# A graph network with a selecting LSTM: layer norm by node tile, and the weight loads and logit stores around the recurrence reordered

## The chip, the cores and the metric

The kernel runs on one core of one Trainium2 chip. The metric is the device time of one execution in microseconds (us), less is better. In the profile PE is TensorE (PEld its weight loads), DVE is VectorE, ACT is ScalarE, POOL is GpSimd and SP is SyncE. A name with a q (SPq, ACTq, POOLq) is the part of that engine which issues DMAs.

## What is computed

Eight residual blocks are applied one after another to a node matrix x of 625 x 512 fp32. Each block takes the layer norm of x over its 512 columns, computes something, and adds the result to x, so that no block can begin its own matmuls before the last one has finished x:

```python
def _layernorm(x, axis=-1, eps=1e-05):
    m = jnp.mean(x, axis=axis, keepdims=True)
    v = jnp.var(x, axis=axis, keepdims=True)
    return (x - m) / jnp.sqrt(v + eps)

x = x + _L0_gnn_ref(_layernorm(x), edge_index, ...)      # Chebyshev graph convolution, 8 terms
x = x + _L0_ffn_ref(_layernorm(x)[None], ...)[0]         # one of 16 experts, chosen by the mean node
x = x + _L1_gnn_ref(_layernorm(x), edge_index, ...)      # weighted graph convolution, 20000 edges
x = x + _L1_ffn_ref(_layernorm(x)[None], ...)[0]         # 8 experts, gates by Sinkhorn, each takes its top 78 nodes
x = x + _L2_gnn_ref(_layernorm(x), ...)                  # 32 relations from 8 bases, sum over 20000 edges
x = x + _L2_ffn_ref(_layernorm(x)[None], ...)[0]         # LSTM over the 625 nodes, 4 weight sets
x = x + _L3_gnn_ref(_layernorm(x), edge_index, ...)      # two graph attention layers
x = x + _L3_ffn_ref(_layernorm(x)[None], ...)[0]         # grouped-query attention, one of 3 variants
```

The sixth block is a recurrence. For each of the 625 nodes in order it picks one of four weight sets by the largest of four logits, which depend on the last hidden state, the last cell state and the node:

```python
def step(carry, x_t):
    h, c = carry
    sel_in = jnp.concatenate([h, c, x_t], axis=-1)
    logits = sel_in @ W_sel.T + b_sel
    onehot = jax.nn.one_hot(jnp.argmax(logits, axis=-1), Sx)
    g_all = x_t @ W_ih.T + h @ W_hh.T + b_ih + b_hh      # for all four sets
    g = jnp.einsum('bsg,bs->bg', g_all, onehot)
    h2, c2 = _lstm_activate(g, c)
    return (h2, c2), h2
```

## The kernel before

The 625 nodes are five tiles of 125 partitions (`P`, `NT`). x stays in SBUF as 125 x 5 x 512 for the whole run. The edges are 160 chunks of 125 (`EC`). The stages are methods called in order: `setup` (which calls `graph`, counting matrices over the edges), then `l0_gnn`, `l0_ffn`, `l1_gnn`, `l1_ffn`, `l2_gnn`, `l2_ffn`, `l3_gnn`, `l3_ffn`, then `store`. A scheduler puts the instructions of each engine in an order of its own and adds the semaphores for what depends on what. Only the regions marked `tc.tile_critical()` are ordered by hand: the loops over edge chunks and the recurrence. Such a region begins when every engine and every transfer before it is done, which the profile shows as a wait of SP (L174, L286, L744, L1038).

**Layer norm.** `layer_norm` (L39 to L55) is called at the head of each stage. It takes bn_stats and bn_aggr of the five tiles on DVE (L46, L47), one square root of 125 x 5 values on ACT (L48), one reciprocal (L49) and five scalings on DVE (L51). The results go to a pool of the stage. `transpose_nodes` (L57 to L64) then turns each tile by four PE transposes (L63) into one PSUM tile, which DVE copies (L64).

**l1_ffn** first asks ACT for eight 1 MB loads of `bases` (L531), for the next stage. It multiplies all nodes by the experts in (expert, tile) products of four fp32 matmuls (L551, `products`). The first five experts' products (`EARLY`) are held in SBUF (`y_early`, L560) while Sinkhorn (L574 and after) and the ranking run. The ranking takes one row of gates per expert through PE (L595) and compares it on DVE (L602, L604). Then each product is scaled by its selected gate and added to x (L620), and with each product of a later expert two held ones are added as well.

**l2_gnn** loads the small combination matrix in sixteen DMAs on ACT (L648), forms the node's eight basis products (L668), combines them to 32 relations (L694) and stores each relation's table to DRAM in 1 MB stores (L703). The relational sum is a hand-ordered region: POOL gathers 125 rows per chunk by an indirect DMA into one of six slots (L748), DVE builds the weighted one-hot matrix (L752), PE sums into five PSUM banks (L216).

**l2_ffn** has two parts. The gate phase computes all gates from the nodes: eight blocks c of W_ih, each as two 1 MB loads on ACT (`load`, L810) into the memory of the fourth recurrent set, `whh[3]`, of which two blocks have room; five tiles each; per (c, t) ten matmuls (L907, L909), then the gates are split into three bf16 summands (`summands`, L797 to L800) and stored to DRAM as `gxp` by SP (L920, 750 KB). Beside it the cell is computed as if each node stood alone (`cell_alone`, `turn`, `parts`), which gives the node's own logits. The recurrent sets 0 to 2 are loaded by SP in twelve 1 MB pieces (`load_set`, L767), one at every odd tile; set 3 by POOL after the last two blocks. At the end the logit rows `xl3` are stored into the last 26 columns of `gxp` by five DMAs of 19 KB on ACT (L938), and the recurrence (L950 on) loads one row of `gxp` per step (`gs`, L1152), adds the recurrent matmuls (L1024) and applies the cell on DVE and ACT.

The `gxp` columns that no logit fills are zeroed by 15 small DMAs on POOL (L92). `store` (L343) writes x with one 1.25 MB DMA.

## Time and profile before

| | |
|---|---|
| runs shown | 5628.12, 5625.29, 5628.01 us; median 5628.01 |
| profiled execution | 5631.39 us, its span 5629.6 us, mean granted TensorE clock 0.946 |
| PE busy | 4921.4 us, 87% of the span |
| DVE busy | 2534.5 us, 45% |
| ACT busy | 1099.2 us, 20% |
| POOL busy | 346.7 us, 6% |
| DMA | 243.7 MB, mean 43 GB/s |

| stretch of the span (us) | what runs |
|---|---|
| 0 to 181 | setup and graph |
| 181 to 505 | l0_gnn |
| 505 to 558 | l0_ffn |
| 558 to 779 | l1_gnn |
| 779 to 976 | l1_ffn |
| 976 to 1208 | l2_gnn to the last relation's table |
| 1242 to 1503 | relational sum |
| 1503 to 1884 | norm and gate phase of l2_ffn |
| 1909 to 5046 | recurrence |
| 5046 to 5391 | l3_gnn |
| 5391 to 5630 | l3_ffn and the store |

The profile is one execution taken by the hardware profiler. A timeline row gives start, length, engine, line of the kernel, operation, output<-input and count; in brackets at its end stands how long the engine had been idle before it, and what it was waiting for. Rows of a queue (ACTq, SPq) have the time that the engine spent on issuing those DMAs, waits included. A row of busy tenths gives one digit for each fortieth of the span.

### The profile page before, as it was taken

The page shows a single profiled execution, that of the slowest core. Times are in us where ns is not written, and L with a number is a line of the kernel's source. Part 1 is how long each engine was busy: PE and PEld are TensorE (multiplying, and loading weights), DVE is VectorE, ACT ScalarE, POOL GpSimd, SP SyncE. Part 2 cuts the span into 40 slices and gives each one's busy share as a digit, 9 for nine tenths or more (in the row PEclk, how much of TensorE's full clock was granted, in tenths as well). Part 3 has the DMA queues.
Part 4 walks back from the last instruction along what each step waited for, and adds up shares of the span by engine and source line. Part 5 has one row for each costly group of instructions (what it writes and reads, how often), then busy time and mean ns, then how long its engine had stood idle before and what let it go on. Part 6 is the DMA issues. An engine that isn't in the chain of part 4 may idle for free.

```text
span 5629.6 us, 171946 instructions
## 1 busy us (share of the span) xinstructions
PE 4921.4 (87%) x73432; PEld 2934.8 (52%) x73433; DVE 2534.5 (45%) x10389; ACT 1099.2 (20%) x3500; POOL 346.7 (6%) x297
## 2 busy tenths in 40 slices
PE   6898678967799699898999999999999898888887
PEld 2444453322344366565666666666666565565543
DVE  6312637234334344444454445444555444456514
ACT  1000731210033111111111111111111111114314
POOL 1000620017500000000000000000000000000000
PEclk8798889979899899999999999999999999999989
DMA  1000121686554200000000000000000000011000
GB/s 15 32 30 12 37 95 38 185 251 166 140 160 146 75 10 11 10 11 10 11 11 10 10 11 11 11 10 10 11 10 11 10 11 10 9 33 38 16 32 10
DMA packets 148634, 243.70 MB, mean 43 GB/s; under 512 B 55035, under 2 KB 57412, under 8 KB 146342
## 3 DMA queue, kind: packets, MB, share of 16 engines
q1 hardware_dynamic: 83850, 163.27, 9.8%
q0 software_dynamic: 45168, 51.96, 3.7%
q10 hardware_dynamic: 19372, 25.52, 1.5%
q8 instruction: 115, 1.88, 0.2%
q14 instruction: 129, 1.06, 0.1%
HBM read 156.40 MB, written 73.72 MB: 41 GB/s over the span
## 4 chain that ended last, share of the span: by engine, by line
PE 54%; DVE 6%; issue 3%; DMA 2%; PEld 1%; ACT 1%; PEldq 0%; SPq 0%; ACTq 0%; DVEq 0%
PE gate_if L1024 22%; PE gate_o L1024 9%; PE gate_g L1024 9%; DVE to L1136 3%; PE gate_if L1015 3%; PE idle L1032 2%; DMA gs<-gxp 2%; PE o_ps L1197 2%; PE o_ps L1263 2%; PE big_ps L1372 1%; PE big_ps L1392 1%; PE gate_g L1015 1%; PE gate_o L1015 1%; PE fc_ps L1303 1%; PE blk_ps L1253 0%
## 5 line engine op out<-in xcount | busy, mean ns | idle before, releaser
L1024 PE MATMUL gate_if<-whh,h 128*32 128x256 f32 x21664 | 1349.6, 388 | 0.0
L1024 PEld LDWEIGHTS gate_if<-whh,h 128*32 128x32 f32 x21664 | 600.1, 109 | 365.6 <-DVE h L1140 129.0
L1024 PE MATMUL gate_g<-whh,h 128*32 128x128 f32 x19968 | 673.9, 275 | 1.5 <-issue 1.5
L1127 DVE STREAM_TRANSPOSE tif<-gate_if 128x256 f32<-128x256 f32 x625 | 281.3, 450 | 840.6 <-PE gate_g L1024 837.1
L1024 PE MATMUL gate_o<-whh,h 128*32 128x128 f32 x19968 | 659.2, 273 | 0.0
L1024 PEld LDWEIGHTS gate_g<-whh,h 128*32 128x32 f32 x19968 | 521.9, 110 | 176.0 <-issue 166.8
L1024 PEld LDWEIGHTS gate_o<-whh,h 128*32 128x32 f32 x19968 | 557.9, 110 | 0.0
L1119 ACT ACTIVATE sd<-tif 128x8 f32<-128x8 f32 x625 | 134.7, 216 | 2124.7 <-DVE tif L1127 2124.7
L1015 PE MATMUL gate_if<-gs,pick 128*128 128x256 bf16 x678 | 192.6, 284 | 138.3 <-DVE to L1136 46.2
L907 PE MATMUL gx_ps<-whh,xT 128*125 128x512 f32 x640 | 299.9, 612 | 0.3 <-DVE xls L847 0.3
L216 PE MATMUL acc<-msg,dst_w 125*125 125x512 f32 x352 | 188.4, 640 | 107.2 <-DMA msg<-rel_table,row_i 94.4
L1128 DVE STREAM_TRANSPOSE tg<-gate_g 128x128 f32<-128x128 f32 x625 | 198.0, 317 | 163.5 <-PE gate_g L1024 163.5
L748 POOL DMA_INDIRECT msg<-rel_table,row_i x160 | 196.5, 1228 | 550.0 <-issue 536.9
L1136 DVE STREAM_TRANSPOSE to<-gate_o 128x128 f32<-128x128 f32 x625 | 197.9, 317 | 66.3
L1084 PE MATMUL logits<-gs,three 128*2 128x5 bf16 x624 | 103.5, 166 | 130.1 <-issue 50.9
L1148 DVE MAX8 mx<-logits 2x8 f32<-2x8 f32 x624 | 101.1, 162 | 248.0 <-PE logits L1096 248.0
L1032 PE MATMUL idle<-hot 128*128 128x384 bf16 x624 | 204.7, 328 | 0.0
L1084 PEld LDWEIGHTS logits<-gs,three 128*2 128x2 bf16 x624 | 49.3, 79 | 291.5 <-DMA gs<-gxp 229.4
L1015 PEld LDWEIGHTS gate_if<-gs,pick 128*128 128x128 bf16 x678 | 65.0, 96 | 227.3 <-DVE to L1136 138.8
L907 PEld LDWEIGHTS gx_ps<-whh,xT 128*125 128x125 f32 x640 | 115.6, 191 | 128.0 <-issue 127.2
L216 PEld LDWEIGHTS acc<-msg,dst_w 125*125 125x125 f32 x352 | 57.3, 192 | 239.1 <-issue 192.6
L752 DVE TENSOR_SCALAR dst_w<-iota,dst,ew 125x625 f32<-125x625 f16 x160 | 106.7, 669 | 160.6 <-PE acc L216 145.3
(377 smaller groups left out, 6380.9 us busy)
## 6 DMA issues: line engine op xcount, KB each, us to landing
rel_table<-h_rel SPq DMA_DIRECT2D x39, 1024.0 KB
gs<-gxp SPq DMA_DIRECT2D x625, 48.6 KB
gxp<-gxo SPq DMA_DIRECT2D x40, 750.0 KB
whh<-in_L_ffn_W_ih ACTq DMA_DIRECT2D x16, 1024.0 KB
whh<-in_L_ffn_W_hh SPq DMA_DIRECT2D x12, 1024.0 KB
node_basis<-by_basis SPq DMA_DIRECT2D x39, 256.0 KB
ch_wk<-in_L_gnn_weight SPq DMA_DIRECT2D x8, 1024.0 KB
expert<-in_L_ffn_experts SPq DMA_DIRECT2D x8, 1024.0 KB
```

The source lines that it names most:

```text
L216: m = PE.matmul(out, lhs, rhs, start=False, stop=False, skip_group_check=True)
L748: get = nc.gpsimd.indirect_dma_start(out=msg[:, i, :], out_offset=None, in_=table, in_offset=bass.IndirectOffsetOnAxis(ap=idx[:, c : c + 1 ...
L907: nc.tensor.matmul(ps[:, q], xT[:, k, t * P : (t + 1) * P], w[:, q, k, :], start=k == 0, stop=False)
L1015: m = PE.matmul(out[:, : hi - lo], pick, gs[:, s * D + lo : s * D + hi], start=True, stop=last, skip_group_check=True)
L1024: yield PE.matmul(out[32 * j : 32 * j + 32, : hi - lo], h[:, b : b + 1].to_broadcast([128, 32]), self.whh[s][:, b, j, lo:hi], start=False, ...
L1032: PE.matmul(idle[:, :cols], hot[:, :128], hot[:, :cols], start=True, stop=True)
L1084: after(PE.matmul(lg[:, :LG], three[:, 0], gs[:, S * D : S * D + LG], start=True, stop=False), s_gx, rows)
L1119: after(ACT.activation(sd[:, :, :, 1], tif.rearrange("p (g b r) -> p g b r", g=2, r=32)[:, :, :, 0], AF.Sigmoid), s_v, 4 * t + 1).then_inc ...
L1127: after(DVE.transpose(tif, IF[:, :256]), s_if, t + 1).then_inc(s_v)
L1128: after(DVE.transpose(tg, G[:, :128]), s_g, t + 1).then_inc(s_v)
L1136: after(DVE.transpose(to, O[:, :128]), s_o, t + 1).then_inc(s_v)
L1197: nc.tensor.matmul(ps[:P, :512], fT[:, c, t * P : (t + 1) * P], w[:, c, :], start=c == 0, stop=c == kc - 1)
```

## The change

It has these parts.

- `layer_norm(pool)` for all tiles becomes `norm(t)` for one, called directly after the tile's last add to x, in the stage before. The square root is of 125 x 1 values. The result lies in `self.xn`, a tensor that lives for the whole run, as do the moments.
- In `l1_ffn` three held products are added beside each later product instead of two.
- The first two blocks of W_ih (4 x 1 MB) are asked for by ACT inside the relational sum, when eight chunks are summed, and ACT waits for them there. Before, ACT asked for the first block's two loads and the second's ahead of the sum.
- In the gate phase each W_hh load is ordered behind the gate store it stands next to. In the order that is built, stores and loads then alternate as store, store, load on SP, from block 0 to block 5, and no W_hh load is left ahead of the sum. Set 3's eight loads of 512 KB go to ACT's queue instead of POOL's.
- The logit rows are stored by POOL in the recurrence's own region, each store waiting for the one before; SP waits for the store of a tile before its first `gs` load (steps 0, 125, 250, 375, 500).
- `rest` and `less` lie in `self.xn`, `b3` shares the memory of `chT`, `sg` and `th` have one buffer instead of two, and `xl3` lives through the recurrence.
- The zeros of `gxp` are asked for in `l1_ffn` in the code. In the order that is built they stand where they stood, at the program's start.
- x is stored by tile, five DMAs of 250 KB, each after its last add.

In the order that is built, the five bias adds of `l2_gnn` (L728) move from before the relational sum to behind it. In `l1_ffn` Sinkhorn's matmuls follow two products without further products between them; eight products stand between the first and the second row of the ranking.

```diff
-    def layer_norm(self, pool):
+    def norm(self, t):
         nc, x = self.nc, self.x
...
+        st, mv, rs = (v[:, t] for v in self.moments)
+        nc.vector.bn_stats(st, x[:, t, :])
+        nc.vector.bn_aggr(mv, st)
+        nc.scalar.activation(rs, mv[:, 1:2], AF.Sqrt, bias=self.eps)
         nc.vector.reciprocal(rs, rs)
+        nc.vector.tensor_scalar(self.xn[:, t, :], x[:, t, :], mv[:, 0:1], rs, op0=ALU.subtract, op1=ALU.mult)
...
+            for t in range(NT):
+                self.norm(t)
             for t in range(NT):
                 nc.scalar.copy(self.count[:, t, :512], main[t])
...
             for e, t, ps in products(range(EARLY, NE)):
                 add(e, t, ps)
-                for _ in range(2):
+                if e == NE - 1:
+                    self.norm(t)
+                for _ in range(3):
                     if held:
...
                         get.then_inc(s_msg[i], 16)
                         hot.then_inc(s_dve)
+                    nc.scalar.wait_ge(s_out, 8)
+                    for i, s in enumerate(s_ih):
+                        nc.scalar.dma_start(*self.w_ih(i // 2, i % 2)).then_inc(s, 16)
+                    for s in s_ih:
+                        nc.scalar.wait_ge(s, 16)
                 for t in range(NT):
                     nc.vector.tensor_add(x[:, t, :], acc[t], x[:, t, :])
+                    self.norm(t)
...
-                    nxt = load(c + 1) if c + 1 < 2 * DC else None
+                    if 1 < c + 1 < 2 * DC:
+                        load(c + 1)
...
-                        nc.sync.dma_start(gxp[t * P : (t + 1) * P, c // 2, :, at : at + 2 * D],
-                                          o3.rearrange("p r s q n -> p r (s q n)"))
+                        put = nc.sync.dma_start(gxp[t * P : (t + 1) * P, c // 2, :, at : at + 2 * D],
+                                                o3.rearrange("p r s q n -> p r (s q n)"))
                         if t % 2:
-                            next(recurrent, None)
+                            with tc.issue_after(put.ins):
+                                next(recurrent, None)
                     if c >= 2 * DC - 2:
-                        list(self.load_set(S - 1, slice(2 * (c % 2), 2 * (c % 2) + 2), nc.gpsimd))
+                        list(self.load_set(S - 1, slice(2 * (c % 2), 2 * (c % 2) + 2), nc.scalar))
...
-                for t in range(NT):
-                    nc.scalar.dma_start(gxp[t * P : (t + 1) * P, 0, :, 4 * D :], xl3[:, :, t])
...
+            for t in range(NT):
+                d = nc.gpsimd.dma_start(gxp[t * P : (t + 1) * P, 0, :, 4 * D :], xl3[:, :, t])
+                if t:
+                    after(d, s_xl, 16 * t)
+                d.then_inc(s_xl, 16)
             for t in range(N):
+                if t % P == 0:
+                    SP.wait_ge(s_xl, 16 * (t // P + 1))
                 d = SP.dma_start(gs[: 3 * DC, :], gxp[t].rearrange("j q g -> (j q) g"))
...
                 nc.vector.tensor_add(x[:, t, :], ps[:, :D], x[:, t, :])
+                nc.sync.dma_start(self.out[t * P : (t + 1) * P, :], x[:, t, :])
...
-    k.store()
```

## The prediction

> **What bounds the kernel now.** The profiled execution took 5631.4 us, 1.8 us of it outside its span of 5629.6; the shown runs have a median of 5628.0, 3.4 below it. Differences are worked out in profile time and taken from both.
>
> I read the chain that ended last, then the row of the granted clock, then the timeline where both dip.
>
> ```profile
> PE 54%; DVE 6%; issue 3%; DMA 2%; PEld 1%; ACT 1%; PEldq 0%; SPq 0%; ACTq 0%; DVEq 0%
> PE gate_if L1024 22%; PE gate_o L1024 9%; PE gate_g L1024 9%; DVE to L1136 3%; PE gate_if L1015 3%; PE idle L1032 2%; DMA gs<-gxp 2%; PE o_ps L1197 2%; PE o_ps L1263 2%; PE big_ps L1372 1%; PE big_ps L1392 1%; PE gate_g L1015 1%; PE gate_o L1015 1%; PE fc_ps L1303 1%; PE blk_ps L1253 0%
> ...
> PEclk8798889979899899999999999999999999999989
> ```
>
> Lines of the recurrence (L1015 to L1152) fill the chain: its first matmul is at 1909.1, its last state at 5046.2, 624 steps of 5.02 us on average (mostly 4.67, by the distances of the DVE's L1127). No compute in a step is edited, so 3137 us stand still. What can move lies in the joints between stages, where PEclk drops, and in the phase before the recurrence. The timeline at those joints:
>
> ```profile
> 779.46 13.25 ACTq L531 DMA_DIRECT2D bases<-in_L_gnn_bases  x8
> ...
> 792.76 0.30 ACT L48 ACTIVATE ln_rs<-ln_mv,eps 125x5 f32<-125x5 f32 x1 [14.98 <-DMA bases<-in_L_gnn_bases]
> ...
> 985.62 0.30 ACT L48 ACTIVATE ln_rs<-ln_mv,eps 125x5 f32<-125x5 f32 x1 [74.23 <-DMA comb<-in_L_gnn_w_comp]
> ...
> 1207.67 8.27 ACTq L810 DMA_DIRECT2D whh<-in_L_ffn_W_ih  x4
> ...
> 1242.30 3.64 DVE L752 TENSOR_SCALAR dst_w<-iota,dst,ew 125x625 f32<-125x625 f16 x6 [15.12 <-issue]
> ...
> 1884.22 15.94 ACTq L938 DMA_DIRECT2D gxp<-xl  x5
> ...
> 1909.14 0.40 PE L1015 MATMUL gate_if<-gs,pick 128*128 128x256 bf16 x1 [27.01 <-DMA gs<-gxp]
> ...
> 5616.56 0.36 SPq L344 DMA_DIRECT2D out<-x  x1
> ```
>
> Twice the one square root of a norm stands on ACT behind DMA issues: eight at 779.5, and sixteen (L648, 8.31 from 977.25), and PE idles 14.6 and 11.3 for it; the relational sum begins 34 us after the last h_rel copy (1207.6 to 1208.1) because its region waits for all transfers, W blocks included; the recurrence begins 27 us after the last gate work; the output goes out as one store after the last add.
>
> **Part by part** (us; minus is saved).
>
> *Setup and graph, +5.* The four norms that now precede the graph loop on DVE cost 4 x 0.66 bn_stats plus aggregates of 0.17, reciprocals of 0.19 and one scaling of 0.54: about 3.8, before a loop that started DVE-bound at 29.9; the table load at 29.46 (1.28) goes ahead of it, -0.5. Behind the loop the other norms stand ahead of the count copies: +1. Nothing covers the first 3.8; if x lands late it is less. Range 0 to +7.
>
> *l0_gnn to l0_ffn, -2.5.* The last matmul ended at 505.1, the 20 mean_ps matmuls at 520.7. Of these, the last 16 (16 x 0.43 = 6.8) now follow the 16 transposes of four finished tiles: end near 518. Range -5 to 0.
>
> *l0_ffn to l1_gnn, -8.5.* PE idled 7.06 until 564.8 (bn chain, then table load 1.28 and sqrt, in series), and the h store left at 575.4. Now 16 transposes of four tiles run at once; only the last tile's add 0.75, bn 0.66, aggregate 0.17, sqrt 0.30, reciprocal 0.19, scaling 0.54 stay: store near 567. The table load lies beside the earlier tiles' matmuls. What is late next is the store itself, unchanged. Range -11 to -5.
>
> *l1_gnn, l1_ffn and into l2_gnn, -19.* Four square roots now go before the bases loads, the last behind two issues of 1.66 at most: the first transpose can follow the last lin_ps at 779.4, sinkhorn starts near 797 instead of 810.5. In the order now built its eight iterations have no product between them (3.43 each for four fp32 matmuls), so the first row is out at about 820 instead of 847.9; but eight products then stand before the second row (8 x 3.43 = 27.5, until about 850), where DVE waits. Ranking stays DVE-bound, 9.13 a row by the ten L602/L604 pairs of 0.87: end near 915 instead of 923. Three held adds per product instead of two put two more adds (0.75) before the first buffer is free; PE's stall, which ended at 929.2, should end near 923.7. So the stage ends 5.5 earlier, not 13.5. Then the square root behind the 16 comb issues: first L668 came 17.4 after the last product; now four tiles are ahead and the fifth is behind one issue (0.52): 20 transposes and the last norm, about 4, so -13.5. Range -26 to -12.
>
> *Entry to the relational sum, -27.* The 4 MB of W_ih and 2 MB of W_hh (issued 1207.7 to 1226) leave the region's front. The windows show what they occupied:
>
> ```profile
> 1215.00:1240.00 25.00, 0.00 (x0) 0.00 (x0) 3.10 (x5) 0.00 (x0) 0.00 (x0) 0.50 0.99 236
> ...
> 1300.00:1350.00 50.00, 35.83 (x67) 9.71 (x66) 22.25 (x33) 0.00 (x0) 39.92 (x34) 1.00 0.64 169
> ```
>
> (length, busy time of PE, PEld, DVE, ACT, POOL, then clock, DMA share, GB/s.) Left are about two 1 MB stores (2.7 each at 353 GB/s), a 64 KB store and a 250 KB load: entry near 1215 instead of 1242.3. The h_rel stores, DMA-bound at a share of 1.0, are then late. Range -30 to -20.
>
> *Inside the sum, +6.* The 4 MB now run beside the gathers, after eight chunks. No row shows that mix. Below: nothing, since the share is 0.64. Above: in the 17 us that 4 MB take at 236 GB/s, gathers get no more than half of what they need: about +16. I take +6, nearer the row, as a third of the share is free. ACT waits here for s_out and four semaphores; behind it stand only the norms' square roots, needed 240 us later.
>
> *After the sum, -5.* Before: adds, bn, one sqrt, then 20 transposes; gates' first matmul at 1524.9, 22.4 after the last sum matmul. Per-tile norms overlap this by some 8; the five bias adds (5 x 0.62 = 3.1), which were hidden at 1224, now stand behind the sum. Range -9 to +1.
>
> *Gate phase, -6.* 40 tiles of 8.385 are PE-bound. The one stall, 5.0 at 1677, is seen here: ACT waits for a store's buffer, the stores being late on SP behind a bias row that sat 11.4 on the queue and a W_hh load.
>
> ```profile
> 1665.58 11.42 SPq L901 DMA_DIRECT2D bih<-bias  x1
> ...
> 1679.92 1.01 ACT L797 CAST gxo<-gx_ps 125x1024 bf16<-125x1024 f32 x1 [9.96 <-DMA gxp<-gxo]
> ```
>
> With W_hh strictly behind its store this should go, with the half clock after it (2.5). Set 3's eight 512 KB issues move from POOL to ACT: SP's unblocked ones took 0.44 to 0.58, so 4 x 0.55 = 2.2 in a tile where ACT is busy some 3.5 of 8.4. Uncovered, they would cost at most 4.4. Range -8 to +3.
>
> *Into the recurrence, -8.* The five 19 KB row stores (L938, 15.9 on ACT's queue) leave; DVE waited 19.6 for them. Next late are the last W_hh loads (POOL's landed in 11.1; issued near 1880, near 1891) and the last gate stores. Then the first row store on POOL: 1.3 issue and 6.0 to land (the row of the same-sized zeros), gs load 1.9: PE starts near 1901 instead of 1909.1. The four others are chained on POOL, where nothing is queued behind, and SP waits for each only at steps 125, 250 and so on, 600 us after it. Range -13 to +2.
>
> *l3_gnn -1* (DVE was busy almost throughout 5047 to 5066, so the same work ends at about the same time; -5 to +2). *l3_ffn -5.5*: the mean ended at 5407.8; now the last tile's norm is done near 5395.5, without the 1.28 table load, and 16 x 0.43 follow: 5402.3 (-8 to -3).
>
> *Output, -8.* From the store's issue to the span's end were 13.0: 1.25 MB at the 128 GB/s of those windows is 10.0, the rest fixed. A 250 KB store takes 2.0 + 3.0 = 5.0. The Trainium skill speaks against splitting: "DMA: Bandwidth & Descriptors", section Rules for kernel authors, says to coalesce many small transfers. By its fit (section on the anatomy of one DMA, about 2.0 fixed plus bytes over 436 GB/s) each piece is 2.6, five are 13 in series. But four lie beneath matmuls 3.43 apart; only the last counts: -8.0 by the row, -10.4 by the rule's price. I take the row, -8.
>
> The zeros for gxp are moved in the code, but in the built order they stand at the same place on POOL: nothing.
>
> Sum: +5 -2.5 -8.5 -19 -27 +6 -5 -6 -8 -1 -5.5 -8 = **-79.5**. Profile time 5551.9; from the median 5548.5.
>
> **Clock.** The Trainium skill's page "TensorE: Matmul & The Clock Gate", section Why this matters for your kernels, says that PE keeps its full clock if idle gaps stay under about 3 us. Today it is 0.50 from 785 to 815, 984 to 996, 1510 to 1539. If the shorter joints kept it up, half of some 24 + 4 + 14 us would go too: up to -21. Against it stands the row at 5050 to 5054: gaps of 1.7 and less between transposes, and the clock fell to 0.50 all the same; the page's part on PE-mode transpose says these do not count as busy alike. The joints are still full of transposes. I take nothing of it.
>
> **Rivals.**
> 1. Contention gives part back: the sum pays +16, the gate stall only moves, the last W_hh hold the recurrence's start. Then 10 + 6 + 8 = 24 of the gain go: 5573. For it: DMA share 0.50 to 0.64 here; against: PE-bound by 8.4 a tile. Chance 0.17.
> 2. The clock stays up in the joints: about -20 more, 5529. Chance 0.10.
> 3. Slower: the recurrence. PE has "issue" gaps of up to 9.3 when a step changes its weight set (steps of 7.2 to 16 instead of 4.67; some 60 of them). If the moved code made each dearer, it decides from 79.5 / 60 = 1.3 a change; at 2.0 the time is 5628 - 79.5 + 120 = 5668. Nothing in the diff touches that code. Chance 0.04.
> 4. The joints' gains fall on the wrong side of other waits nearly altogether, within 0.2% (11 us, what this kernel's measurement can tell): 0.02.
>
> The forecast itself has 0.67. Faster 0.67 + 0.17 + 0.10 = 0.94. For the range, the parts' own bounds rarely add up in one direction; about 25 each way, widened to rivals 1 and 2: 5520 to 5590.
>
> **What would show it.** Square roots (125x1) before the bases loads; no idle above 5 near 976; the sum entered near 1190 (1242 less the 52 of the parts ahead of it), PE waiting on msg some 67 us instead of 94; no ACT wait of 10 for gxp; the recurrence's first matmul about 65 earlier than 1909; steps of 4.67; the last store landing within 5 of its issue. Wrong it would be if steps lengthen, if gathers wait for W_ih beyond 16, or if the ranking waits on the eight products.

## The result, and the profile after

The changed kernel took **5570.91 us** (median of 5581.44, 5572.16, 5563.39, 5569.67) beside 5626.65 for the kernel before, measured together with it (5620.61 to 5628.12): a ratio of 0.9901, 95% interval 0.9889 to 0.9912. It is faster by 1%, in the foreseen direction and within the foreseen range, but by 56 us where the forecast said 79; part of these 56 came from where nothing was forecast, as the table below shows. The profiled execution took 5581.4, with a span of 5579.7.

The page of the changed kernel, from the chain that ended last (shares by engine, then by line), and above it the row of the granted clock:

```profile
PEclk8799789979899899999999999999999999998999
...
PE 53%; DVE 6%; issue 3%; DMA 2%; PEld 1%; ACT 1%; PEldq 0%; SPq 0%; DVEq 0%; POOLq 0%; ACTq 0%
PE gate_if L1023 21%; PE gate_o L1023 9%; PE gate_g L1023 9%; DVE to L1135 3%; PE gate_if L1014 3%; DMA gs<-gxp 2%; PE idle L1031 2%; PE o_ps L1269 2%; PE o_ps L1203 2%; PE big_ps L1399 1%; PE big_ps L1379 1%; PE gate_o L1014 1%; PE gate_g L1014 1%; PE fc_ps L1309 1%; PE blk_ps L1259 0%
```

The chain has the same composition as before: the recurrence fills it. The timeline of the changed kernel at the joints whose rows of before stand in the prediction:

```profile
776.69 0.29 ACT L45 ACTIVATE ln<-ln,eps 125x1 f32<-125x1 f32 x1 [1.04 <-DVE ln L44]
...
781.26 10.29 ACTq L524 DMA_DIRECT2D bases<-in_L_gnn_bases  x6
...
975.60 0.29 ACT L45 ACTIVATE ln<-ln,eps 125x1 f32<-125x1 f32 x1 [3.79 <-DVE xT L56]
...
1202.39 3.53 DVE L754 TENSOR_SCALAR dst_w<-iota,dst,ew 125x625 f32<-125x625 f16 x6 [6.12 <-DMA bias<-in_L_gnn_h_bias]
...
1221.20 4.27 ACTq L763 DMA_DIRECT2D whh<-in_L_ffn_W_ih  x4
...
1891.97 1.33 POOL L1151 DMA_DIRECT2D gxp<-xl  x1 [406.44 <-issue]
...
1897.85 0.40 PE L1014 MATMUL gate_if<-gs,pick 128*128 128x256 bf16 x1 [29.51 <-DMA gs<-gxp]
```

The square roots are no longer held behind the bases or comb issues (14.98 and 74.23 before; 1.04 and 3.79 now), and the relational sum is entered at 1202.4 instead of 1242.3. But the first matmul of the recurrence comes at 1897.9, only 11.2 earlier than before: most of a lead of 39.9 was lost between these two rows.

Where the time went, by the distances between PE matmuls that border the stages (us). *Again* is a second profile of the same changed kernel, described below. The row of the edge sums holds work that was forecast to stay as it is.

| from … to | before | predicted | after | again |
|---|---|---|---|---|
| start to the first product of l0_ffn | 532.4 | +2.5 | -3.9 | -2.0 |
| to the first edge sum of l1_gnn | 54.6 | -8.5 | -5.6 | -4.2 |
| edge sums and L511, to the last `lin_ps` | 191.8 | 0 | +7.5 | +1.5 |
| last `lin_ps` to the first bases product | 214.1 | -19 | -12.0 | -13.0 |
| to the first matmul of the relational sum | 255.9 | -27 | -25.4 | -26.9 |
| relational sum | 253.2 | +6 | **+16.0** | **+14.9** |
| to the first gate matmul | 22.9 | -5 | -0.7 | -0.7 |
| gate phase | 351.5 | -6 | **+10.0** | -1.8 |
| to the first recurrence matmul | 32.7 | -8 | **+2.9** | **+3.9** |
| recurrence | 3132.0 | 0 | -20.6 | -34.0 |
| l3_gnn | 349.9 | -1 | -3.0 | -3.3 |
| l3_ffn to the last output matmul | 224.2 | -5.5 | -7.5 | -7.1 |
| last matmul to the end of the span | 14.4 | -8 | -7.6 | -7.6 |
| sum (the span) | 5629.6 | -79.5 | -49.9 | -80.3 |

The parts that were predicted to change gave -36.8 and -47.7, not -79.5. That *again* ends at -80.3 all the same comes from the recurrence (-34.0), for which nothing was forecast: no computation of a step was edited, though the logit stores and five waits of SP now stand in its region.

### The profile page after: what moved, and what is told of

It reads as the page before. It is cut to its first block, busy times and chain, and to the rows that moved or that the text cites. A ratio compares the mean times of both kernels' runs of the same rounds, so it can differ in the third digit from the quotient of the medians.

```text
span 5579.7 us, 172066 instructions
## 1 busy us (share of the span) xinstructions
PE 4923.3 (88%) x73432; PEld 2926.8 (52%) x73433; DVE 2543.5 (46%) x10421; ACT 1108.5 (20%) x3531; POOL 353.5 (6%) x294
## 4 chain that ended last, share of the span: by engine, by line
PE 53%; DVE 6%; issue 3%; DMA 2%; PEld 1%; ACT 1%; PEldq 0%; SPq 0%; DVEq 0%; POOLq 0%; ACTq 0%
PE gate_if L1023 21%; PE gate_o L1023 9%; PE gate_g L1023 9%; DVE to L1135 3%; PE gate_if L1014 3%; DMA gs<-gxp 2%; PE idle L1031 2%; PE o_ps L1269 2%; PE o_ps L1203 2%; PE big_ps L1399 1%; PE big_ps L1379 1%; PE gate_o L1014 1%; PE gate_g L1014 1%; PE fc_ps L1309 1%; PE blk_ps L1259 0%
## 5 line engine op out<-in xcount | busy, mean ns | idle before, releaser
L1126 DVE STREAM_TRANSPOSE tif<-gate_if 128x256 f32<-128x256 f32 x625 | 281.6, 450 | 851.8 <-PE gate_g L1023 826.1
L1127 DVE STREAM_TRANSPOSE tg<-gate_g 128x128 f32<-128x128 f32 x625 | 198.2, 317 | 162.3 <-PE gate_g L1023 162.3
```

What stands on the lines that cost most here:

```text
L1126: after(DVE.transpose(tif, IF[:, :256]), s_if, t + 1).then_inc(s_v)
L1127: after(DVE.transpose(tg, G[:, :128]), s_g, t + 1).then_inc(s_v)
```

## The experiments

All kernels but *before again* start from the changed kernel. Rivals for the missing 43 us (32 in *again*): contention (the 4 MB beside the gathers, stores and loads on one queue), the order of work that was built (Sinkhorn without products), the joints themselves being worth less than their rows, or mere variation between executions.

### Variation: the two kernels once more

> The changed kernel once more, unaltered. Asked: is what its first profile showed outside the edited places repeatable? There the edge loop of l1_gnn (first to last matmul into its sums) took 176.1 us instead of 168.7, and the recurrence 3113.7 us over 624 steps instead of 3134.3, with 8 steps over 9 us instead of 11. Theory A (execution noise): the loop comes back to 168 to 172 or moves again, the number of long steps differs from 8, and the time falls between 5563 and 5582. Theory B (the change shifts code and thereby both): loop 176 and 8 long steps again, within 1 us.

> The kernel before once more, unaltered, for its profile. The changed kernel's recurrence took 3111, 3098, 3118, 3118 and 3128 us in five profiles of it and its variants, the kernel before's 3132 in one. Theory A (the number of steps that wait on PE's own issue differs from execution to execution in both kernels): the recurrence falls anywhere from 3098 to 3135. Theory B (the change made these waits rarer): 3130 to 3135, as 7 shown runs within 5624 to 5635 suggest.

The changed kernel gave 5553.92 (5551.07 to 5576.87), ratio 0.9881 (0.9858 to 0.9904); over both measurements its eight executions have a median of 5566.5. That is a wider spread than the 5563 to 5582 expected of noise; the edge loop of l1_gnn came back as expected (171.2 from first to last matmul, after 177.2). The kernel before, run as an experiment, took 5640.99 once, 5624.54 beside it. By the distances of DVE's transposes of the forget and input gates (L1127 before, L1126 after), 563 to 566 of 624 steps are under 6 us in all four profiles and take 4.67; what differs is how many steps are over 9 us: 11 and 9 before, 8 and 6 after (138.6, 123.1, 99.4 and 77.8 us). They recur at the same steps (1, 3, 84, 133, 499, 572 …), not in every execution. What comes with them can be read from the DMA packets: in all fourteen profiles each step over 9 us has at least one 16 KB packet on q8, the queue that the profile calls instruction, and no step without such a packet takes over 7.4. There are 39 of these packets in the recurrence of *again* (3098.0), 48 in *after* (3111.4) and 59 in *before* (3132.0). So the long steps go with loads of program code; why their number differs was not tried. Over the twelve profiles of the changed kernel and its variants the recurrence took 3098.0 to 3135.6, in the two of before 3132.0 and 3129.7. So a single profile's total says little about 20 us, and the stages outside the recurrence have to be compared by their own distances. Whether the change makes long steps rarer stays open: two profiles of before are too few, and variants of the changed kernel have 59 packets too.

### The order of Sinkhorn (sink)

```diff
-                            nc.tensor.matmul(ps, xT[:, c, t * P : (t + 1) * P], w[:, c, :],
-                                             start=c == 0, stop=c == DC - 1)
+                            self.last = nc.tensor.matmul(ps, xT[:, c, t * P : (t + 1) * P], w[:, c, :],
+                                                         start=c == 0, stop=c == DC - 1)
...
-            for _ in range(ITERS):
+            for i in range(ITERS):
...
+                with tc.issue_after(self.last.ins) if i else ExitStack():
```

(the iteration's matmuls are ordered behind the product written before them, so that products stand between the iterations again)

> The eight Sinkhorn iterations get one product each between them again, by issue order alone. Theory 1 (the joint before l1_ffn did gain 12.5 us, and lost it because Sinkhorn ran with PE nearly idle, at half clock, while the eight products it had covered then kept the ranking waiting 20 us): Sinkhorn lasts about 36 instead of 27 us, the 20 us wait of DVE ahead of the second row is gone, the last product ends about 10 us earlier than in the changed kernel, total -8 to -12. Theory 2 (ranking and products are bound by PE in sum, whatever the order): last product within 2 us of the changed kernel's, total unchanged.

The changed kernel's timeline in Sinkhorn and at the second row of the ranking:

```profile
804.67 1.91 PE L570 MATMUL small_ps<-gates,ones 125*125 125x8 f32 x10 [1.22 <-DVE gates L577]
807.81 2.27 PE L570 MATMUL small_ps<-gates,ones 125*125 125x8 f32 x10 [1.23 <-DVE gates L577]
811.30 2.27 PE L570 MATMUL small_ps<-gates,ones 125*125 125x8 f32 x10 [1.22 <-DVE gates L577]
...
822.97 28.93 PE L547 MATMUL y_ps<-expert,xT 128*125 128x512 f32 x64
...
853.25 0.87 DVE L598 TENSOR_SCALAR_CACHE_REDUCE scratch<-row,gates 125x625 bf16<-125x625 f32 x1 [20.18 <-ACT row L595]
```

Iterations follow one another every 3.49 us (2.48 while the clock was still up, by the starts at 802.19 and 804.67), as the ten small matmuls take 2.27 instead of 1.16. Then 64 matmuls hold PE for 28.93 while DVE, which bounds this part, waits 20.18 for the next row. In *sink* products fill the waits:

```profile
800.02 1.16 PE L571 MATMUL small_ps<-gates,ones 125*125 125x8 f32 x10
801.03 3.68 PE L547 MATMUL y_ps<-expert,xT 128*125 128x512 f32 x8
...
824.17 0.87 DVE L599 TENSOR_SCALAR_CACHE_REDUCE scratch<-row,gates 125x625 bf16<-125x625 f32 x1 [3.72 <-ACT row L596]
```

Sinkhorn itself is longer (33.1 instead of 24.1), but rows 1 to 8 of the ranking follow in 52.3 instead of 74.9, and from the last `lin_ps` to the last product it takes 182.9 instead of 195.8 and 194.8 (before: 196.2). So the new order of PE's work was giving back some 12 us: not by Sinkhorn itself, which it makes shorter even at half the clock, but by the products that it puts between the first two rows. The time, 5560.68 (ratio 0.9883, 0.9867 to 0.99), cannot be told from *again*; its recurrence took 3117.8.

### Where the W_ih blocks are asked for (wih_front, wih_tail)

Front: the four loads are issued ahead of the sum's region (all four at 1186.7 to 1194.4 in the trace, though the expectation has two of them behind the sum). Tail: behind the last square root after the sum.

```diff
-                    nc.scalar.wait_ge(s_out, 8)
-                    for i, s in enumerate(s_ih):
-                        nc.scalar.dma_start(*self.w_ih(i // 2, i % 2)).then_inc(s, 16)
-                    for s in s_ih:
-                        nc.scalar.wait_ge(s, 16)
                 for t in range(NT):
                     nc.vector.tensor_add(x[:, t, :], acc[t], x[:, t, :])
-                    self.norm(t)
+                    root = self.norm(t)
+                with tc.issue_after(root.ins):
+                    for i in range(4):
+                        nc.scalar.dma_start(*self.w_ih(i // 2, i % 2))
```

> The four W_ih loads stand ahead of the relational sum in the code; in the order built, block 0's two are asked for there and block 1's two behind the sum. Theory C (4 MB beside the gathers cost the 16 us by which the sum is longer; ten chunks took 20.7 and 24.2 us instead of 15.3 there): the sum from first to last matmul is 253 again instead of 268 to 269, its start comes 8 to 9 us later (2 MB at 243 GB/s), and the gates start 22 us behind it as before: net -5 to -8 at the first gate matmul. Rival (the sum is longer because it starts beside the last relation stores and a cold PE): it stays above 263.

> The four W_ih loads are asked for by ACT behind the last norm after the sum, where the queues are idle. Theory C: the sum is 253 again, its start is unchanged, and 2 MB at 243 GB/s (8.6 us and some 2 to land) fit into the about 14 us between the last square root and the first gate matmul: net -13 to -16 at the first gate matmul. Rival (the loads become the wait): the gates' start slips by up to 10 us, net -5.

The changed kernel's stretches of 15 us from the first matmul of the sum on (length, busy time and records of PE, PEld, DVE, ACT, POOL, then clock, DMA share, GB/s):

```profile
1209.40:1224.40 15.00, 12.61 (x20) 3.98 (x20) 6.23 (x9) 0.00 (x0) 12.08 (x10) 0.82 0.64 175
1224.40:1239.40 15.00, 8.26 (x10) 2.07 (x10) 3.36 (x6) 0.00 (x0) 8.21 (x8) 0.66 1.07 272
1239.40:1254.40 15.00, 8.86 (x10) 2.60 (x11) 2.69 (x5) 0.00 (x0) 7.00 (x5) 0.59 1.01 211
1254.40:1269.40 15.00, 12.34 (x22) 4.03 (x21) 7.06 (x11) 0.00 (x0) 11.42 (x9) 0.84 0.50 137
```

and of the run wih_tail:

```profile
1195.10:1210.10 15.00, 13.07 (x20) 4.04 (x20) 6.74 (x10) 0.00 (x0) 11.95 (x11) 0.80 0.59 170
1210.10:1225.10 15.00, 10.91 (x20) 2.93 (x20) 7.66 (x10) 0.00 (x0) 11.95 (x11) 1.00 0.59 168
1225.10:1240.10 15.00, 10.97 (x21) 2.93 (x20) 8.51 (x11) 0.00 (x0) 11.94 (x11) 1.00 0.58 172
```

Undisturbed, a stretch has 20 matmuls and POOL asks for 10 chunks. With W_ih under way the DMA engines are full (1.07 and 1.01) for two stretches, and each has 10 matmuls: 30 us at half the pace is 15 us lost, which is what the sum lost. With the loads elsewhere it took 253.8 (front) and 253.1 (tail), as before the change. In front they delay the first matmul of the sum instead: 235.9 from the first bases product instead of 230.5, so 10 of the 15 are kept (beside *again*, 8). Behind the sum the first gate matmul came 22.2 after the last of the sum, as with the loads already done, so the delay that their landing might have brought did not show there; the gate phase was 364.1, within 3 of *after* and 14 above *again*. The times (5567.71 and 5577.7, one each) lie within the variation; tail's recurrence was the longest of all, 3135.6.

### The gate stores and the W_hh order (whh_free, split, split_bih)

whh_free takes the order off:

```diff
                         if t % 2:
-                            with tc.issue_after(put.ins):
-                                next(recurrent, None)
+                            next(recurrent, None)
```

> The order of W_hh behind the gate stores is taken off; the scheduler then asks for two of the 1 MB pieces ahead of the relational sum (one of them before its transfers are waited for) and for most others before or early in the gate phase. Theory Q (SP's queue order makes the stall): PE's waits in the gate phase fall from about 13 us to 5 or less, phase about 10 us shorter; the sum is entered 4 to 9 us later; total -6 to +2. Theory E (five engines full in sum over the phase): waits in the gate phase are about as long as in the changed kernel in blocks where a W_hh load is left, total 0 to +9.

It took 5593.34 (ratio 0.9933, 0.9917 to 0.995), longer than the changed kernel. The way from the bases to the sum was 9.1 longer (239.6; 10.6 beside *again*), since W_hh loads stand ahead of the sum again. The gate phase was 352.3, still with one stall of 5.7 as before, and the last gate matmul to the recurrence took 3 to 4 less. So for the entry to the sum the order is worth having. But all stages outside the recurrence add to 2455.5, between *after* (2461.5) and *again* (2444.5): that the whole is 22 to 39 longer is not shown to come from the order.

split stores each tile as 112 rows and 13:

```diff
-                        put = nc.sync.dma_start(gxp[t * P : (t + 1) * P, c // 2, :, at : at + 2 * D],
-                                                o3.rearrange("p r s q n -> p r (s q n)"))
+                        for lo, hi in ((0, 112), (112, P)):
+                            put = nc.sync.dma_start(gxp[t * P + lo : t * P + hi, c // 2, :, at : at + 2 * D],
+                                                    o3[lo:hi].rearrange("p r s q n -> p r (s q n)"))
```

> Each gate store of 125 rows is made of two, of 112 and 13 rows; nothing else. In the changed kernel a store alone on the queues shows 117 GB/s at a DMA share of 0.33. Theory E (a store of 125 rows uses five of the sixteen engines, 6.4 us of every 8.4, and with 4 MB of weights in each block these five are full): share and rate of a lone store rise about twofold or more, PE's waits of 2.2 to 5.7 us in the gate phase vanish, phase shorter by about 15 us, and the last store lands some 5 us earlier, total -15 to -22. Theory Q (the stores are late because they stand behind W_hh loads on SP's queue while W_ih drains): at most half of the stalls go, total -3 to -10.

ACT's waits in the gate phase of the changed kernel (us in total, times, longest):

```profile
ACT sg L872 <- PE gx_ps L910: 125.8, 33, 18.1
ACT gxo L807 <- DMA gxp<-gxo: 67.7, 19, 10.7
```

and its SP queue and PE around one of these waits:

```profile
1764.60 11.26 SPq L921 DMA_DIRECT2D gxp<-gxo  x2
1775.90 11.79 SPq L775 DMA_DIRECT2D whh<-in_L_ffn_W_hh  x1
1787.78 9.46 SPq L921 DMA_DIRECT2D gxp<-gxo  x2
...
1793.45 0.60 PE L884 MATMUL ch_ps<-identb,ch 125*128 125x125 bf16 x4 [5.74 <-DVE ch L876]
```

The W_hh issue holds SP for 11.79. Issues of the same form took 0.31 to 6.78 in the profile of before. While it stands there the next store cannot be issued, ACT waits for a store's buffer (67.7 us in all, 53.6 in *again*, 35.8 before), and PE stalls for ACT's and DVE's cell work: four times, 12.2 in all in *after*, against once 5.0 before. But in *again*, the same kernel, the issues are as long and PE hardly waits:

```profile
1671.86 12.17 SPq L775 DMA_DIRECT2D whh<-in_L_ffn_W_hh  x1
...
PE ch_ps L884 <- DVE ch L876: 3.3, 3, 2.3
```

A long issue alone, then, does not make the stall. With this order and whole stores the phase is about 350 in three profiles (*again*, *sink*, *norm_head*; PE waits 2.7 to 3.6) and 361 to 364 in five (*after*, *wih_front*, *wih_tail*, *combo*, *combo_last*; 11.1 to 13.9). What decides between the two stays open. The difference itself is accounted for: after the phase's start the clock was at half for 10.2 us in *after* and 3.4 in *again*, which costs, as an estimate, half of that; with the waits this makes 17.3 and 5.0, and the phases differ by 11.8.

In *split* the waits of ACT for stores are gone from the list and the W_hh issues took 0.34 to 1.61 us. But PE waits for something else:

```profile
PE gx_ps L910 <- DMA bih<-bias: 15.9, 3, 6.5
```

The bias rows, asked for two at a time and late on SP, held PE three times, and the phase grew to 368.7, where 15 less had been expected; the time was 5574.9 (ratio 0.9902, 0.9886 to 0.9919). In the other place split did what it should: last gate matmul to first recurrence matmul 23.5 instead of 35.6. Asking for the bias rows on POOL cured only the named wait:

```diff
-                    nc.sync.dma_start(b, bias3.rearrange(
+                    nc.gpsimd.dma_start(b, bias3.rearrange(
```

> Gate stores in two pieces of 112 and 13 rows as in the run split, and the bias rows of the gate phase asked for by POOL instead of SP. In split ACT no longer waited for stores at all, but PE waited 3.9, 6.5 and 5.5 us for bias rows that stood late on SP's queue, and the phase took 368.7 us. Theory E (the five engines were the cause of the store waits, the bias rows an accident of SP's order): no wait over 2.2 us between first and last gate matmul, phase 338 to 343 (40 tiles of 8.4 and the slow clock at its start), recurrence again 23 to 24 us after it. Rival (DMA as a whole is too busy, bias rows are late from any queue): phase above 350.

No wait for bias rows was left, yet the phase was 376.2 and the time 5593.58 (one execution). PE now waits for DVE's subtraction of the summand (L808, seven times, 8.7 in all) and for small steps of the cell (6.7). These waits are short, but the clock fell with them. From 1677.4 to 1831 it has a mean of 0.91, and in the same stretch of *again* 0.99:

```profile
1677.40:1831.00 153.60, 142.36 (x395) 58.91 (x394) 52.76 (x77) 49.88 (x78) 1.12 (x2) 0.91 0.55 150
...
1677.40:1831.00 153.60, 150.29 (x464) 63.08 (x463) 55.53 (x87) 55.32 (x87) 0.00 (x0) 0.99 0.55 167
```

It was at half six times there, 27.3 us in all: an estimated 13.7 lost beside the 15.4 of waits, which makes 29.1 against the 5.0 of *again*, of a difference of 26.5. The order in which DVE and PE take the tiles was built differently in this kernel, so this is not the same program with one wait less; why DVE was late was not separated further.

### The norm at the stage's head again (norm_head)

```diff
-                    self.norm(t)
...
+            for t in range(NT):
+                self.norm(t)
             xn = self.xn
             xT = pool.tile([128, DC, N], F32, name="xT")
```

(the calls in l1_gnn and l1_ffn are taken out, and the loop stands at the head of l1_ffn and of l2_gnn; each norm is still of one tile. Three of the five square roots then stand behind the bases issues again, one behind the comb issues)

> The norms ahead of l1_ffn and l2_gnn are called at the head of those stages again, tile by tile; in the order built three square roots stand behind the eight bases loads and one behind the sixteen comb loads. Theory 1 (those joints gain 12.5 and 11.6 us, and the first gain is lost again by Sinkhorn's order): last lin_ps to first Sinkhorn matmul about 31 instead of 17 to 19, last product to first basis product 13 to 17 instead of 6.3; but from last lin_ps to last product no more than 5 us more than the changed kernel's 195, if the products move back between the iterations. Theory 2 (the square roots wait in any case for DVE): both joints within 3 us of the changed kernel's.

Last `lin_ps` to the first Sinkhorn matmul 22.8 instead of 19.3 and 17.3, last product to first bases product 13.2 instead of 6.3: norms called with each tile's last add are worth 3.5 to 5.5 and 6.9 in these joints. Before it was 31.7, and about 31 was expected here: most of the first joint's gain comes from a norm of one tile at a time, wherever it is called. The last product was nevertheless 182.1 after the last `lin_ps`, as in *sink*, because in this kernel's built order the products are back between the iterations. So where the norm is called changes, through the order that is built, what stands between the iterations; the 12 us are of that order, not of the norms themselves. 5562.68, one execution.

### All together (best, combo, combo_last)

best is sink + split + bias rows on POOL + wih_tail; combo is sink + wih_tail; combo_last adds the split for the stores of the last block alone:

```diff
+                        for lo, hi in ((0, 112), (112, P)) if c == 2 * DC - 1 else ((0, P),):
```

> The changed kernel with one product between Sinkhorn iterations, W_ih asked for behind the sum, gate stores in pieces of 112 and 13 rows and bias rows on POOL. If the parts add up: -13 (Sinkhorn) -15 (sum) -7 to -18 (gate phase) -13 (last stores ahead of the recurrence) against the changed kernel, 5500 to 5525 us with the recurrence between 3098 and 3136; ratio to the kernel before 0.977 to 0.982. If W_ih becomes the wait behind the sum or the stores' pieces crowd SP, 5530 to 5550.

> The Sinkhorn order of run sink (products back between the iterations) and the W_ih blocks asked for behind the last square root of the relational sum as in run wih_tail; stores and bias rows as in the changed kernel. If the two joints are separate, as their rows say, it saves what both saved: last lin_ps to last product near 183 instead of 195, last sum matmul 253 after the first instead of 268, first gate matmul near 1466 instead of 1494 to 1501. The gate phase is then 350 to 364 and the entry to the recurrence 34 to 37, as in the runs with whole stores; about 27 below the changed kernel, 5535 to 5545. If, against that, the 4 MB asked for at the end of the sum come late into the first gate tiles, the gate phase is above 364 and at most 15 is left.

> Run combo with the stores of the last block alone (five of the forty) in 112 and 13 rows. If the last stores, draining through a third of the DMA engines, hold the first step, last gate matmul to first recurrence matmul falls from 34 to 37 to 23 or 24 while the gate phase stays that of run combo within 4: 10 to 13 below run combo. If it is the number of pieces in the whole phase that counts, it stays above 30 and the time is run combo's.

| | time | ratio to before | gate phase | to recurrence | recurrence | all else to the last matmul |
|---|---|---|---|---|---|---|
| after | 5570.91 | 0.9901 (0.9889 to 0.9912) | 361.5 | 35.6 | 3111.4 | 2461.5 |
| again | 5553.92 | 0.9881 (0.9858 to 0.9904) | 349.7 | 36.6 | 3098.0 | 2444.5 |
| best | 5561.63 | 0.9875 (0.9857 to 0.9892) | 372.8 | 23.2 | 3124.5 | 2426.4 |
| combo | 5564.47 | 0.9897 (0.988 to 0.9913) | 363.3 | 34.6 | 3127.0 | 2427.2 |
| combo_last | 5553.23 | 0.987 (0.9854 to 0.9887) | 360.9 | 23.5 | 3129.6 | 2418.9 |

(stage columns from the one profile of each; the last is the last output matmul less the recurrence, 2483.2 and 2495.1 for the two profiles of before)

Best missed what was expected of it (5500 to 5525, or 5530 to 5550 with a rival): its gate phase was the second longest of all. In combo each joint came as foreseen (last product 182.2 after `lin_ps`, sum 254.5, first gate matmul at 1464.0), yet the time missed 5535 to 5545 by 20: the gate phase stood at the upper end, and the recurrence was 15.6 and 29 longer than in *after* and *again*. combo_last saved 11.2 more, at the place foreseen. The changed kernel between its last gate matmul and the recurrence:

```profile
1862.30:1879.00 16.70, 3.04 (x23) 1.77 (x21) 6.49 (x23) 3.73 (x7) 0.00 (x0) 0.63 0.73 184
1879.00:1886.00 7.00, 0.00 (x0) 0.00 (x0) 0.00 (x0) 0.00 (x0) 0.00 (x0) 0.50 0.32 115
1886.00:1898.00 12.00, 0.15 (x1) 0.13 (x2) 0.00 (x0) 0.00 (x0) 2.64 (x2) 0.50 0.11 22
```

and combo_last:

```profile
1830.70:1842.70 12.00, 2.87 (x23) 1.65 (x21) 6.51 (x23) 3.73 (x7) 0.00 (x0) 0.70 0.99 214
1842.70:1854.20 11.50, 0.04 (x1) 0.04 (x2) 0.00 (x0) 0.00 (x0) 2.63 (x2) 0.50 0.26 72
...
1843.00:1845.00 2.00, 0.00 (x0) 0.00 (x0) 0.00 (x0) 0.00 (x0) 0.00 (x0) 0.50 0.93 325
```

From 1879 to 1886 no engine works, and the transfers left use a third of the DMA engines (0.32, 115 GB/s): the last stores of 125 rows. With 112 and 13 rows the engines are full beside the W_hh loads (0.99), and from 1843 to 1845, when those are done and the store is alone, it moves 325 GB/s at a share of 0.93. The first step comes 11.1 to 12.1 sooner. The Trainium skill has the rule for it ("DMA: Bandwidth & Descriptors", section "Why a DMA increments its semaphore by 16 and not by 1"): a DMA runs on the largest number of engines up to 16 that divides its outer dimension on both sides. For 125 that is 5, and five of sixteen are 0.31, beside the 0.32 measured; for 112 it is 16, for 13 it is 13. Nothing in the prediction used it, though the output store that it did price, at 128 GB/s, had the same share (0.33 in the trace of before).

combo_last has the lowest stages outside the recurrence, some 64 below the first profile of before and 26 below *again*, and is faster than before; that it beats the changed kernel is not shown by the times, since *again* has the same median.

## The prediction, step by step

**Right.** Direction and range. The square roots ahead of the bases loads, no idle of PE above 0.84 before the l2_gnn products near 976, the l2_gnn joint (11.6 less of 13.5), the entry to the sum (-25.4 of -27), l3_ffn and the output (-7.6 of -8; the span ends 5.5 after the last store's issue, 5.0 foreseen), steps of 4.67. In the output the row (-8), not the price of -10.4, was what came; that price is an estimate from a fit which the Trainium skill's page gives for transfers issued by GpSimd, and these are issued by SP. To take nothing for the clock was right after the sum, where it was at half for 34.1 us before and after. Near 980 it was not: 3.4 us of half clock instead of 17.1. That it fell there at all, with no idle above 0.84, is another case in which the Trainium skill's rule on gaps ("TensorE: Matmul & The Clock Gate") does not keep the clock up by itself; transposes stand there, as at the row of 5050.

**Luck.** The parts that were forecast to change gave 36.8 and 47.7. With 36.8 alone the time would be 5591, just outside the range; the recurrence, of which nothing was expected, brought it inside. And the first rival's 5573 was met within 2 us although its parts add to 55.5.

**Wrong, and which term.** The forecast of 5549 took the likeliest case to be the one without contention. Much of the first rival, "Contention gives part back", happened instead: the sum paid all of it, the recurrence's start was held, though by another transfer, and the gate stall moved in one profile and nearly went in the other. It was given 0.17 and deserved more. The terms:

- *Inside the sum, +6*: measured +16.0 and +14.9. The step "nearer the row, as a third of the share is free" failed. The free third is an average at the gathers' own pace; the four loads, all asked for in 4.3 us, filled the DMA engines for 30 us and halved the gathers. The upper bound of +16 was met, but not by its working: half pace over 17 us loses 8.5. It lasted 30 us, and half of that is 15.
- *l1_ffn, the stage's -5.5*: measured about 0 (-0.4 and -1.4). The stage began 2.0 earlier, so its rows count 2.0 later in the time of before: first row at 823.8 (820 foreseen), second at 855.3 (850). The ranking was done 3.3 earlier within the stage, where 8 was foreseen. The rest went to the five later x updates and products: first update 6.8 after the ranking instead of 5.5, and 104 matmuls in 47.9 instead of 46.3, as the clock was at half for the first 6.2 us of them instead of 3.0.

```profile
929.22 46.34 PE L551 MATMUL y_ps<-expert,xT 128*125 128x512 f32 x104 [11.59 <-DVE x L620]
...
925.25 47.93 PE L547 MATMUL y_ps<-expert,xT 128*125 128x512 f32 x104 [11.16 <-DVE x L616]
```

  The larger point was seen and priced as given, not questioned: eight products ahead of the second row cost 12, as *sink* shows.
- *After the sum, -5*: measured -0.7. The term that failed is the overlap of 8. The transposes waited for the last add to x (8.0 idle; 8.6 before), not for a norm:

```profile
1483.64 0.53 DVE L47 TENSOR_SCALAR xn<-x,ln,ln 125x512 f32<-125x512 f32 x1
...
1486.47 0.66 DVE L767 TENSOR_TENSOR x<-acc,x 125x512 f32<-125x512 f32 x1
...
1487.18 1.09 PE L55 MATMUL tr_ps<-ident,xn 125*128 125x125 f32 x4 [8.03 <-DVE x L767]
```

  The first tile's norm was done at 1484.2, 3.0 before. Then the 40 small matmuls for the logits (8.4) were in series as before. The 3.1 for the bias adds were not paid: they ran at 1472.0 to 1475.2, beneath the last matmuls of the sum. That the PSUM of the sums has to be read before the transposes can write is a reading of that wait, not tried.
- *Gate phase, -6*: measured +10.0 and -1.8. "With W_hh strictly behind its store this should go" failed: behind its store the load's issue takes up to 12.65 and holds the next store. In *after* the stall moved and multiplied (12.2 instead of 5.0); in *again* 3.3 were left. Why the two differ stays open.
- *Into the recurrence, -8*: measured +2.9 and +3.9. "Next late are the last W_hh loads" named the wrong transfer: it was the last gate stores, on a third of the engines. The row store did land in 2.6, quicker than the 6.0 taken.
- *Setup, +5*: measured +1.9 to the first degree matmul (the second profile of before: +1.5 without any change), and l0_gnn then gave it back; too cautious by 6. Its items for the norms, each taken four times, add to 4.6 and not to 3.8; with that the +5 comes out.

The third rival, steps becoming dearer, did not come; the recurrence was shorter in both profiles, with fewer loads of program code; whether the change has a part in that stays open.

## What to carry to other kernels

When a load is moved under other work, ask what that work's DMA share becomes during the transfer, not on average: four 1 MB loads asked for together took all DMA engines here for 30 us, and the gathers beside them ran at half their pace. When a transfer is ordered behind a store on one queue, look at how long its issue holds that queue: it was up to 12.65 us here, and the next store came that much later. And look at the order that was built after a change: where fillers were moved out of a chain of small matmuls, they stood in front of the next stage's first need, and that stage lost what the joint had saved.

## What the runs showed of the hardware

- A store of 125 rows, alone, uses about a third of the DMA engines (0.32, 115 GB/s); one of 112 and 13 rows, alone, moves 325 GB/s at a share of 0.93. The one output store of before, 125 partitions too, had 128 GB/s.
- The issue of a 1 MB load on SP took 0.52 to 12.65 us in *after*, where each stands behind a gate store, 0.31 to 6.78 before, and 0.34 to 1.61 with the stores in 112 and 13 rows.
- At half clock ten matmuls of 125x8 take 2.27 instead of 1.16, and the clock fell within a chain of them with gaps of 1.2 us, and stayed down to the end of the chain (805 to 821).
- In the gate phase waits of PE of 1.2 to 2.3 us, close together, came with a clock at half for 27.3 us (*split_bih*).
- Long steps of the recurrence come at fixed step numbers but not in every execution, 6 to 11 of them over 9 us. Each has a 16 KB packet on the instruction queue. Their sum differed by up to 67 us between profiles (77.8 to 144.9), the whole recurrence by 37.5.
